# The last 32 keys of four attention units in one batch of scores

## The chip, the cores and the metric

The kernel runs on one core of one Trainium2 chip. What counts is the device time of one execution in microseconds (us), the median of several runs.

## What is computed

Eight images of 256 channels and 32 × 32 positions pass through three layers: an attention over pooled keys and values, a second attention over the tokens, and a gated sum of eight expert networks. Only the first matters here. Each image has 1426 keys at four pooling levels (1024 + 256 + 121 + 25), 8 heads of 32 channels, and 1024 queries:

```python
ks_ = _layernorm(pooled(k_map).transpose(0, 2, 1), norm_w, norm_b)
vs_ = _layernorm(pooled(v_map).transpose(0, 2, 1), norm_w, norm_b)
k = ks_.reshape(B, N, HEADS, DH).transpose(0, 2, 1, 3)
v = vs_.reshape(B, N, HEADS, DH).transpose(0, 2, 1, 3)
attn = jax.nn.softmax(jnp.einsum('bhqd,bhkd->bhqk', q_g, k) * SCALE, axis=-1)
out_att = jnp.einsum('bhqk,bhkd->bhqd', attn, v)
```

All arithmetic is in float32.

## The kernel before

**Units and chunks.** The function `attention` works image by image. An image is four units: two groups `c` of four heads, times two halves of 512 queries. A unit goes through the keys in chunks of `KEY_CHUNKS` (line 44): eleven of 128 keys and one of 18. One chunk is one step, 8 × 4 × 12 = 384 steps in all.

**A step.** `scores` (line 1463) makes four matmuls, one for each head, in four groups of 32 rows of TensorE's array, since a head has 32 channels. They fill the PSUM tile `sc` of four banks, of which there is one. ScalarE writes its exp to a tile `pt` in SBUF, with six buffers. One step later, `values` (line 1473) makes four matmuls in four groups of 32 columns, which add the chunk's part to the PSUM tile `pv`. After every second chunk, `add` (line 1485) lets a DMA on GpSimd's queue add the odd chunk's exp to the even one's in SBUF; VectorE sums these pairs in `sums` (line 1492), and a matmul with ones makes the softmax's denominators of the result.

**What fills TensorE.** While ScalarE does the exp, TensorE works on other things: projections, transposes and the depthwise convolutions' inputs of the next image, and the second attention (`layer1`) of the image before. They are generators, run by a small planner, the class `Flow`. It keeps its own clock for each engine from a table of costs (`cost`), records the instructions in the order in which it runs the generators, and ties them to that order on each engine. After each step it gives out `PACE` us of TensorE time to the first group of generators and `PACE1` to the second (lines 30 and 31, `step` on line 850). `finish` runs whatever is needed until a condition holds, so that a step has its keys, queries and values.

**Keys and values.** `by_tokens` (line 1252) turns four chunks of a map so that tokens lie on partitions, and normalises them; `key_tokens` (line 1427) turns the keys back into `kn`, channels on partitions, three parts for an image. The values remain as `vt`, one tile for every four chunks, so the chunks' borders are those of `KEY_CHUNKS`.

**The main loop** (from line 1812) takes step after step: scores of step `i`, values of step `i - 1`, and filler in between and after. The list it goes through is

```python
steps = [(b, c, half, kc) for b in range(nb) for c in range(2) for half in range(2) for kc in range(NKC)]
```

After the attention, `experts` runs with what is left of `layer1`. Two functions, `layer0_general` and `layer1_general`, stand ready for inputs whose scores are out of bounds; they aren't executed here. Nearly every instruction in the profile has line 669, that of the planner's wrapper, so groups are told apart by tiles: `sc`, `pt`, `pv`, `vt`, `kn`, `q`.

Of the kernel before, what the change touches and what calls it, by code (L numbers as in the profile page):

```python
# [10 lines left out]
AF = mybir.ActivationFunctionType  # L11
# [15 lines left out]
SCALE0 = DH ** -0.5  # L27
SCALE1 = C ** -0.5
FILLER = 5
PACE = 4.0  # L30
PACE1 = 2.0
CAP = (1.5, 1.5)
NEVER = 1e9
MARGIN = 1.5
# [5 lines left out]
NBOUND = 64  # L40
NSTAGED = 64
LIMIT = 1e12
KEY_CHUNKS = [(i * P, min(P, NK - i * P)) for i in range(NKC)]
KEY_SLICES = [(0, 512), (512, 512), (1024, 402)]


# [96 lines left out]
def layer0_general(tc, kit, nb, x, t1, consts, consts8, vecs, q_t, kv_t, proj_t, gqk_t):  # L143
    nc = tc.nc
    T = kit.tile
    with ExitStack() as ctx:
# [189 lines left out]
        def transpose_values(b):  # L336
            acc = vs.pop(b)
            for i in range(0, NKC, 2):
                ps = T(psum, [P, 512], "sm")
                part = KEY_CHUNKS[i : i + 2]  # L340
                for u, (k0, w) in enumerate(part):
                    for c in range(2):
                        o = u * C + c * P
                        nc.tensor.transpose(ps[:w, o : o + P], acc[:, c, k0 : k0 + w], ident)
                whole = [part] if part[-1][1] == P else [part[:1], part[1:]]
                u = 0
                for group in whole:
                    w, g = group[0][1], len(group)
                    src = ps[:w, u * C : (u + g) * C].rearrange("p (a j d) -> p a j d", j=2, d=DH)
                    dst = vext[:w, i + u : i + u + g].rearrange("p u a s d -> p (u a) s d")  # L350
                    nc.vector.tensor_copy(dst[:, :, 0, :], src[:, :, 0, :])
                    nc.scalar.copy(dst[:, :, 2, :], src[:, :, 1, :])
                    u += g

        def global_token(b):
# [19 lines left out]
            yield  # L375
            yield
            ps = T(psum, [P, 512], "sm")
            for kc, (k0, w) in enumerate(KEY_CHUNKS):
                nc.tensor.transpose(ps[:w, kc * 8 : kc * 8 + 8], pg[:, k0 : k0 + w], ident[:HEADS, :HEADS])
            pt = T(work, [P, NKC * 8], "gpt")  # L380
            last, lw = (NKC - 1) * 8, KEY_CHUNKS[-1][1]
            nc.vector.tensor_copy(pt[:, :last], ps[:, :last])
            nc.vector.tensor_copy(pt[:lw, last:], ps[:lw, last : last + 8])
            yield
            yield
            ps = T(psum, [P, 512], "sm")
            for kc, (k0, w) in enumerate(KEY_CHUNKS):
                nc.tensor.matmul(
                    ps[:HEADS, :C],
                    lhsT=pt[:w, kc * 8 : kc * 8 + 8],  # L390
                    rhs=vext[:w, kc, :, 0::2, :],
                    start=kc == 0,
                    stop=kc == NKC - 1,
                )
# [144 lines left out]
        def attend(n, background, steps):  # L539

            pair = n % 4
            qa, ka = qaug.pop(n), kaug[n % 3]
            av = T(work, [P, HW], "av")
            for half in range(2):
                sl = slice(half * 512, half * 512 + 512)
                pv = T(psum, [P, 512], "pv")
                late = None

                def values(kc, w, pt):
                    for j in range(2):  # L550
                        nc.tensor.matmul(
                            pv[64 * j : 64 * j + 64, :],
                            lhsT=vext[:w, kc, pair, j : j + 2, :].rearrange("p s d -> p (s d)"),
                            rhs=pt[:w, j, :],
                            start=kc == 0,
                            stop=kc == NKC - 1,
                        )

                for kc, (k0, w) in enumerate(KEY_CHUNKS):
                    t = T(psum, [P, 2, 512], "sc")  # L560
                    for j in range(2):
                        rows = slice(64 * j, 64 * j + DH + 1)
                        nc.tensor.matmul(
                            t[:w, j, :], lhsT=ka[rows, k0 : k0 + w], rhs=qa[rows, sl], start=True, stop=True
                        )
                    pt = T(work, [P, 2, 512], "pt", bufs=3)
                    nc.scalar.activation(pt[:w], t[:w], AF.Exp, scale=SCALE0)
                    if late is not None:
                        values(*late)
                    late = kc, w, pt  # L570
                    advance(background, steps)
                values(*late)
                nc.vector.tensor_copy(av[:, sl], pv)
            return av
# [81 lines left out]
class Flow:  # L656
# [54 lines left out]
    def cost(self, engine, op, out, ins):  # L711
# [9 lines left out]
        if engine == "PE":  # L721
            if op == "transpose":
                return 0.13
            c = max(0.2, 0.00169 * n)
            return c if self.tiling(ins) is None else c / 4
        psum = any(i.space == PSUM for i in ins)
        if engine == "ACT":
# [150 lines left out]
        return need[0] is not None and (need[2] is None or self.free(need[2]) < NEVER)  # L878


def attention(tc, kit, f, outer, ended, nb, consts, x, t1, t2, hn, bounds, vecs, q_t, kv_t, proj_t, gqk_t, wqk, wqkv, vecs1, w1_d, w1c, gate_d, wrc, vecs2, bnvec):

# [3 lines left out]
    with ExitStack() as ctx:  # L888
# [159 lines left out]
            f.ve.tensor_tensor(bias, ps[:, 0:2], vec[:, V_PB : V_PB + 2], ALU.add)  # L1048

        ks, qs, vts = {}, {}, {}  # L1050
        made = [0]
        turn = [-1]
        todo, done, read, freed, key_parts, normalised = [], [], [4], [0], [0], [0]
# [13 lines left out]
        def until(cond):  # L1067
            return None, cond, None
# [183 lines left out]
        def by_tokens(accs, dst, k0):  # L1252
# [4 lines left out]
            for i in range(0, 4, 2):  # L1257
                span = slice(chunks[i][0], sum(chunks[i + 1]))
                yield pe(*(acc[:, span] for acc in accs), tag="sm")
                ps = small()  # L1260
                for u, (o0, w) in enumerate(chunks[i : i + 2]):
                    for c in range(2):
                        o = u * C + c * P
                        f.pe.transpose(ps[:w, o : o + P], accs[c][:, o0 : o0 + w], ident)
                w = chunks[i + 1][1]
                if w == P:
                    f.act.activation(dst[:, i : i + 2, :], ps.rearrange("p (u c) -> p u c", u=2), AF.Copy)
                else:
                    f.act.activation(dst[:, i, :], ps[:, :C], AF.Copy)
                    f.act.activation(dst[:w, i + 1, :], ps[:w, C:], AF.Copy)  # L1270
            yield ve(dst)
            for u, (_, w) in enumerate(chunks):
                f.ve.bn_stats(st[:w, u, :], dst[:w, u, :])
# [153 lines left out]
        def key_tokens(b, g):  # L1427
# [7 lines left out]
            for c in range(2):  # L1435
                if g == 0:
                    yield until(lambda: turn[0] >= 2 * b - 2 + c)
                    ks[b, c] = T(work, [P, NK], "kn", bufs=3)
                    f.split(ks[b, c], 512, HW)
                yield pe(kt, tag="sm")  # L1440
                ps = small()
                for u, (_, tw) in enumerate(KEY_CHUNKS[4 * g : 4 * g + 4]):
                    f.pe.transpose(ps[:, u * P : u * P + tw], kt[:tw, u, c * P : (c + 1) * P], ident[:tw, :tw])
                f.act.activation(ks[b, c][:, s0 : s0 + w], ps[:, :w], AF.Copy)
            key_parts[0] += 1

# [16 lines left out]
        def scores(b, c, sl, kc):  # L1463
# [6 lines left out]
            f.act.activation(pt[:w], t[:w], AF.Exp, scale=SCALE0)  # L1470
            return pt

        def values(b, c, kc, pt, pv):
            w = KEY_CHUNKS[kc][1]
            for j in range(4):
# [16 lines left out]
        def sums(n, pairs):  # L1492

            for i in range(1, NKC // 2):
                yield until(lambda: len(pairs) > i)
                for j in range(0, 4, 2):
                    s = pairs[0][:, j : j + 2, :]
                    yield ve(s, pairs[i])
                    f.ve.tensor_tensor(s, s, pairs[i][:, j : j + 2, :], ALU.add)
            yield until(lambda: normalised[0] == n)  # L1500
            yield pe(pairs[0], tag="sm")
            total = small()
# [306 lines left out]
        f.finish(lambda: key_parts[0] > 0)  # L1809
        f.spawn(chain(mix(), weights1(), outputs()), 5)  # L1810
        f.spawn(layer1(), 6)
        steps = [(b, c, half, kc) for b in range(nb) for c in range(2) for half in range(2) for kc in range(NKC)]

        pts = {}
        for i in range(len(steps) + 1):
            if i < len(steps):
                b, c, half, kc = steps[i]
                sl = slice(half * 512, half * 512 + 512)
                if kc % 4 == 0:
                    f.finish(lambda: key_parts[0] > 3 * b + kc // 4)  # L1820
# [5 lines left out]
                    f.finish(lambda: {0, 1}.issubset(whole))  # L1826
                if b == 0 and kc == 0:
                    f.finish(lambda: (c, half) in asked)
                pts[i] = scores(b, c, sl, kc)
                f.step()  # L1830
            if i:
                b1, c1, half1, kc1 = steps[i - 1]
                if kc1 == 0:
                    pv = T(psum, [P, 512], "pv")
                    pairs = []
                    sl1 = slice(half1 * 512, half1 * 512 + 512)
                    f.spawn(unit(b1, c1, sl1, i // NKC, pairs), 0)
                f.finish(lambda: kc1 // 4 in vts[b1])
                values(b1, c1, kc1, pts[i - 1], pv)
                if kc1 % 2:  # L1840
                    add(kc1, pts.pop(i - 1), pts[i - 2])
                    pairs.append(pts.pop(i - 2))
                if kc1 == NKC - 1:
                    f.finish(lambda: projected[0] >= b1)
                    f.act.activation(atts[b1, c1][:, sl1], pv, AF.Copy)
# [509 lines left out]
def tile_conv_attn_hybrid(  # L2355
# [45 lines left out]
    with ExitStack() as early:  # L2401
# [3 lines left out]

        ended = [0]
        attention(
            tc, kit, f, (l1, shared), ended, nb,
            consts, x, t1, t2, hn, bounds, vecs0, q_t, kv_t, proj_t, gqk_t, wqk, wqkv, vecs1, w1_d, w1c, gate_d, wrc, vecs2, bnvec,
        )  # L2410
        last(f, (l1, shared), ended, early)
# [122 lines left out]
```

## Time and profile before

The median is 3326.88 us of three runs (3324.67 to 3327.84). The profiled execution spans 3332.1 us.

| engine | busy us | share of the span |
|---|---|---|
| PE (TensorE matmul) | 3137.4 | 94% |
| DVE (VectorE) | 2472.4 | 74% |
| ACT (ScalarE) | 1734.4 | 52% |
| POOL (GpSimd) | 1227.3 | 37% |

The first attention's steps run from 80 to 1970 us, the experts from there to the end. A group line reads: line, engine, operation, output and input tiles, shapes, count, then busy time in us and mean ns of one, then idle time ahead of them and what ended it. `32*128` at a matmul means rows times columns of the array in use. A matmul in float32 is two records. Busy shares are averages over stages with different limits, so they are read by stage.

### The profile page before, as it was taken

Reading aid. Unit: us, or ns where it says so; the run is one execution under the profiler, and the core shown is the slowest. Engines: PE = TensorE matmul, PEld = TensorE weight load, DVE = VectorE, ACT = ScalarE, POOL = GpSimd, SP = SyncE. Lnnn points to the kernel's source line nnn. Section 1 sums busy time; section 2 is a strip of 40 time slices with the busy share of each in tenths; the row PEclk is TensorE's granted clock in tenths of the full one; section 3 lists DMA queues with packets and bytes.
Section 4 is the critical chain, followed back from the end, with each engine's and each line's share of the span. In section 5 each row is a group of like instructions: output and inputs, shape, how many; then the busy total and the mean of one; then the engine's idle time right before and its main releaser. Section 6 shows DMA issues by size and latency. Waiting matters only on the chain.

```text
span 3332.1 us, 42942 instructions
## 1 busy us (share of the span) xinstructions
PE 3137.4 (94%) x15970; PEld 1912.8 (57%) x15970; DVE 2472.4 (74%) x4069; ACT 1734.4 (52%) x2328; POOL 1227.3 (37%) x1300
## 2 busy tenths in 40 slices
PE   8687899999999999899899999999999999999997
PEld 4332244344344344344345346777888888888886
DVE  5687788786887886886884555446998787787776
ACT  4476676666576566576566543333233444444442
POOL 2211413213213214213211112006666776777775
PEclk9798999999999999999999999999999999999999
DMA  2357656656646646656556656124442010000000
GB/s 74 82 121 158 131 106 146 133 101 154 133 100 157 135 104 147 135 120 123 121 125 133 133 119 237 70 88 159 158 146 102 20 45 26 20 20 32 20 13 21
DMA packets 106666, 347.10 MB, mean 104 GB/s; under 512 B 13056, under 2 KB 38408, under 8 KB 83216
## 3 DMA queue, kind: packets, MB, share of 16 engines
q0 software_dynamic: 28608, 179.85, 28.1%
q1 hardware_dynamic: 74480, 162.45, 14.1%
q8 instruction: 128, 2.10, 0.3%
q10 hardware_dynamic: 3360, 1.97, 0.2%
q14 instruction: 90, 0.74, 0.1%
HBM read 105.11 MB, written 73.97 MB: 54 GB/s over the span
## 4 chain that ended last, share of the span: by engine, by line
PE 57%; DVE 5%; issue 3%; ACT 3%; POOL 3%; DMA 2%; SPq 0%; DVEq 0%; POOLq 0%; ACTq 0%
PE bank L669 18%; PE sm L669 13%; PE y L669 8%; PE sc L669 6%; PE sx L669 6%; PE pv L669 5%; DVE h L669 2%; ACT pt L669 2%; POOL tm L669 1%; DVE u L669 1%; DMA pt<-pt 1%; ACT h L669 1%; POOL t L669 1%; DVE t L669 1%; DVE c L669 1%
## 5 line engine op out<-in xcount | busy, mean ns | idle before, releaser
L669 ACT ACTIVATE pt<-sc 128x2048 f32<-128x2048 f32 (+1 forms) x384 | 719.9, 1875 | 326.5 <-PE sc L669 272.7
L669 DVE SCALAR_TENSOR_TENSOR acc<-p,vec,acc 128x225 f32<-128x225 f32 (+7 forms) x928 | 526.6, 574 | 29.3 <-ACT acc L669 4.8
L669 PE MATMUL sc<-q,kn 32*128 32x512 f32 (+1 forms) x3072 | 445.6, 650 | 94.7 <-ACT pt L669 92.9
L669 DVE TENSOR_TENSOR pt<-pt,pt 128x1024 f32<-128x1024 f32 x320 | 387.4, 1254 | 144.3 <-DMA pt<-pt 135.3
L669 POOL DMA_DIRECT2D pt<-pt x192 | 174.0, 907 | 780.1 <-ACT pt L669 615.7
L669 PE MATMUL pv<-pt,vt 128*32 128x512 f32 (+1 forms) x3072 | 420.6, 620 | 0.0
L669 ACT ACTIVATE p1c<-bank 128x256 f32<-128x256 f32 x228 | 87.2, 383 | 576.4 <-PE bank L669 576.1
L669 ACT ACTIVATE h<-h,bnvec 128x512 f32<-128x512 f32 x456 | 345.0, 805 | 50.7 <-DVE h L669 43.7
L669 POOL TENSOR_TENSOR rstd<-rstd,mhalf 128x4 f32<-128x4 f32 (+2 forms) x88 | 107.0, 1216 | 673.8 <-DVE rstd L669 635.0
L669 DVE TENSOR_TENSOR h<-p1c,bank 128x512 f32<-128x512 f32 x228 | 155.2, 681 | 194.7 <-PE bank L669 191.2
L669 PEld LDWEIGHTS sc<-q,kn 32*128 32x128 f32 (+1 forms) x3072 | 116.1, 178 | 285.8 <-ACT pt L669 184.9
L669 POOL TENSOR_TENSOR tm<-h,tm 128x256 f32<-128x256 f32 x206 | 247.6, 1202 | 16.1
L669 DVE TENSOR_TENSOR h<-u,bank 128x256 f32<-128x256 f32 x456 | 232.1, 550 | 7.9
L669 PEld LDWEIGHTS pv<-pt,vt 128*32 128x32 f32 (+1 forms) x3072 | 60.7, 108 | 301.7 <-issue 290.3
L669 POOL TENSOR_TENSOR tm<-h 128x512 f32<-128x512 f32 x103 | 133.9, 1300 | 245.2 <-ACT h L669 241.2
L669 DVE TENSOR_TENSOR h<-h,gate 128x1024 f32<-128x1024 f32 x128 | 209.1, 1642 | 2.5 <-DMA h<-h 2.1
L669 PE MATMUL bank<-h,w2e 128*128 128x256 f32 (+1 forms) x612 | 198.8, 453 | 4.1 <-DVE h L669 4.1
L669 PE MATMUL y<-t,s3e 128*128 128x256 f32 x768 | 188.0, 381 | 10.6 <-POOL t L669 10.3
L669 POOL TENSOR_TENSOR t<-h,t 128x256 f32<-128x256 f32 x210 | 177.4, 845 | 16.5
L669 PE MATMUL bank<-t,s1e 128*128 128x256 f32 x750 | 182.3, 379 | 0.0
L669 PE MATMUL sm<-y,t 128*128 128x256 f32 x752 | 180.6, 385 | 0.0
L669 DVE TENSOR_TENSOR u<-h,bank 128x512 f32<-128x512 f32 x228 | 156.7, 687 | 24.0
(316 smaller groups left out, 5604.3 us busy)
## 6 DMA issues: line engine op xcount, KB each, us to landing
pt<-pt POOLq DMA_DIRECT2D x160, 1024.0 KB, 7.4
h<-h SPq DMA_DIRECT2D x90, 512.0 KB, 3.2
xi<-in_x_dram SPq DMA_DIRECT2D x16, 512.0 KB, 6.7
t<-t SPq DMA_DIRECT2D x8, 1024.0 KB, 9.7
res<-t SPq DMA_DIRECT2D x32, 256.0 KB, 3.9
t<-res SPq DMA_DIRECT2D x32, 256.0 KB, 5.4
hn<-res SPq DMA_DIRECT2D x32, 256.0 KB, 3.0
hn<-hn SPq DMA_DIRECT2D x16, 512.0 KB, 4.2
```

The source lines that it names most:

```text
L669: ins = fn(*args, **kwargs)
```

## The change

The last chunk has only 18 keys and costs a whole step. The change makes the last chunk 32 keys and the one ahead of it 114, and computes the last chunk's scores for all four units of an image at once, in unit 0's last step. There 16 matmuls of 32 rows and 32 columns use every combination of row group (head) and column group (unit), so that the four units' scores lie on four groups of 32 partitions of one `sc` tile. One exp serves them all. Unit 0 uses its part from SBUF. The parts of units 1 to 3 are stored to DRAM tiles `last0` to `last2`, and each is fetched to partitions 0 to 31 of a `pt` buffer when its unit is at its third last chunk. Units 1 to 3 then have 11 steps instead of 12, and the last one makes the values of both its chunks. The rest follows from that: the planner's paces rise to 4.3 and 2.15, its cost of the 16 matmuls is a sixteenth each, the functions that never run keep the old chunks as `WHOLE_CHUNKS`, and sums take only the rows of a pair.

```diff
-PACE = 4.0
-PACE1 = 2.0
+PACE = 4.3
+PACE1 = 2.15
...
-KEY_CHUNKS = [(i * P, min(P, NK - i * P)) for i in range(NKC)]
+WHOLE_CHUNKS = [(i * P, min(P, NK - i * P)) for i in range(NKC)]
+LAST = 32
+KEY_CHUNKS = [(i * P, P) for i in range(NKC - 2)]
+KEY_CHUNKS += [((NKC - 2) * P, NK - LAST - (NKC - 2) * P), (NK - LAST, LAST)]
...
+            if self.key(out).startswith("sc") and ins[0].shape[-1] == LAST:
+                return c / 16
...
+        lasts = [kit.tile(dram, [LAST, 4, 512], f"last{n}") for n in range(3)]
...
+        def last_scores(b):
+            k0 = KEY_CHUNKS[-1][0]
+            t = T(psum, [P, 4, 512], "sc")
+            for n in range(4):
+                c, half = divmod(n, 2)
+                for j in range(4):
+                    r = slice(DH * j, DH * j + DH)
+                    f.pe.matmul(
+                        t[LAST * n : LAST * n + LAST, j, :],
+                        lhsT=ks[b, c][r, k0:],
+                        rhs=qs[b, c][r, half * 512 : half * 512 + 512],
+                        start=True,
+                        stop=True,
+                    )
+            pt = T(work, [P, 4, 512], "pt", bufs=6)
+            f.act.activation(pt, t, AF.Exp, scale=SCALE0)
+            for n in range(1, 4):
+                f.sp.dma_start(lasts[n - 1], pt[LAST * n : LAST * n + LAST])
+            return pt
+
+        def fetch_last(n):
+            pt = T(work, [P, 4, 512], "pt", bufs=6)
+            f.sp.dma_start(pt[:LAST], lasts[n - 1])
+            return pt
...
-                    s = pairs[0][:, j : j + 2, :]
+                    s = pairs[0][:w, j : j + 2, :]
...
-        steps = [(b, c, half, kc) for b in range(nb) for c in range(2) for half in range(2) for kc in range(NKC)]
+        steps = [
+            (b, n, kc) for b in range(nb) for n in range(4) for kc in range(NKC if n == 0 else NKC - 1)
+        ]
...
-                pts[i] = scores(b, c, sl, kc)
+                if kc == NKC - 1:
+                    f.finish(lambda: (b, 1) in qs and (b or len(asked) == 4))
+                    pts[n, kc] = last_scores(b)
+                else:
+                    pts[n, kc] = scores(b, c, sl, kc)
+                if n and kc == NKC - 3:
+                    pts[n, NKC - 1] = fetch_last(n)
                 f.step()
...
-                values(b1, c1, kc1, pts[i - 1], pv)
-                if kc1 % 2:
-                    add(kc1, pts.pop(i - 1), pts[i - 2])
-                    pairs.append(pts.pop(i - 2))
+                for kc1 in (kc1, NKC - 1) if n1 and kc1 == NKC - 2 else (kc1,):
+                    f.finish(lambda: kc1 // 4 in vts[b1])
+                    values(b1, c1, kc1, pts[n1, kc1], pv)
+                    if kc1 % 2:
+                        add(kc1, pts.pop((n1, kc1)), pts[n1, kc1 - 1])
+                        pairs.append(pts.pop((n1, kc1 - 1)))
```

## What the prediction was

> **What bounds the kernel now.** I read the time line of the span in 40 slices first, then busy time by stage, then the groups of instructions with their shapes kept apart, the views of the tiles `sc` and `pt`, TensorE's order of work in one stretch, and the DMA issues.
>
> ```profile
> PE   8687899999999999899899999999999999999997
> DVE  5687788786887886886884555446998787787776
> ACT  4476676666576566576566543333233444444442
> ```
>
> ```profile
> 1043.00:1283.00 240.00, 231.94 (x1321) 109.44 (x1320) 195.21 (x348) 156.82 (x193) 59.91 (x72) 1.00 0.60 130
> 1283.00:1526.00 243.00, 232.66 (x1318) 108.92 (x1320) 194.47 (x349) 156.06 (x193) 61.92 (x72) 0.99 0.58 124
> 1976.00:3332.00 1356.00, 1309.47 (x5782) 1088.48 (x5781) 987.22 (x1409) 496.25 (x821) 760.32 (x737) 0.99 0.21 74
> ```
>
> The columns are span, then busy time of PE, weight load, DVE, ACT and POOL, then clock, DMA share and GB/s. An image of the first attention takes about 240 us, of which PE works 232 (97%), DVE 195 (81%), ACT 157 (65%). ACT, which loses most of the work below, is not the limit; PE is, and DVE is next. The experts after 1976 us are PE-bound as well, and the change doesn't touch their formulas.
>
> ```profile
> 508.27 1.14 PE L669 MATMUL sc<-q,kn 32*128 32x512 f32 x8
> 509.34 1.06 PE L669 MATMUL pv<-pt,vt 128*32 128x512 f32 x8
> 510.33 1.99 PE L669 MATMUL sx<-y,t 128*128 128x256 f32 x8
> 512.26 1.07 PE L669 MATMUL sm<-pt,con 128*32 128x512 f32 x8
> ```
>
> This is one step of `attention`: scores from 508.27 to 509.34 (1.07 us), values to 510.33 (0.99), filler (here layer 1's) after that. Eight records are four matmuls, two passes each. Filler of this shape takes 1.73 us when more of its kind follows (the chain of waits has such pieces), 1.93 here, so a change into full-array work and out of it costs 0.20.
>
> ```profile
> L669 PE MATMUL sc<-q,kn x3072: 587/599/1218, 79.9 to 1968.6; 32*128 32x512 f32 x192
> ...
>   DMA pt<-pt: 17.5, 9
> ...
>   PE sc L669: 92.9, 92
> ```
>
> 3072 records are 384 steps in 1889 us, 4.92 us each. In the list of what ended idle time before work on `sc`, a DMA on a `pt` buffer accounts for 17.5 us, 9 times (exps that had no buffer); in the list of who waited, PE's scores stood 92.9 us for `sc` to be read, less than 5% of the stage.
>
> ```profile
> L669 ACT ACTIVATE pt<-sc 18x2048 f32<-18x2048 f32 x32 | 59.7, 1864 | 27.6 <-PE sc L669 24.3 <-issue 2.9 <-DVE acc L669 0.4
> L669 PE MATMUL sc<-q,kn 32*18 32x512 f32 x256 | 34.0, 600 | 12.6 <-ACT pt L669 12.6
> ```
>
> The last 18 keys cost what 128 cost: exp 1864 ns against 1876, matmul 600 ns against 655. That is the waste the change goes for.
>
> ```profile
> pt<-pt POOLq DMA_DIRECT2D x160, 1024.0 KB, 7.4
> ...
> res<-t SPq DMA_DIRECT2D x32, 256.0 KB, 3.9
> ...
> hn<-pool SPq DMA_DIRECT2D x28, 256.0 KB, 2.8
> ```
>
> An addition of one chunk's exp into its neighbour takes 7.4 us to land, a 256 KB load 3.9, a 256 KB store 2.8.
>
> [...] The trace shows four concurrent, in rows and in columns (1.07 and 0.99 us for four); no run here shows sixteen. [...]
>
> **The change part by part.**
>
> *Removed steps.* Units 1 to 3 of each image lose their last step: 8 × 3 = 24 score batches and 24 exps. PE saves 24 × 1.07 = 25.7 us. The values of those keys remain, but now directly behind those of chunk 10, in the same tiling, and the removed step's filler joins filler elsewhere. I take 0.3 us per step for that: 0.20 for the change into filler and out[...]. 24 × 0.3 = 7.2, so PE loses 32.9 us. ACT loses 24 × 1.876 = 45 us, which lies beside PE and counts for nothing by itself.
>
> *The common batch.* Unit 0's last step becomes 16 matmuls of 32 × 32 with 512 columns. If all run together, 1.07 us plus small start offsets, the cost of the batch it replaces. If the four groups of units run one after the other, 4 × 1.07 = 4.28. [...] I take 1.3, since four distinct operands are already streamed at once today, by the values: 8 × 0.23 = 1.8 us lost. The ends are 0 and 8 × 3.21 = 25.7.
>
> *DRAM round trip.* 48 transfers of 256 KB, 12.6 MB, beside some 236 MB that 125 GB/s make over 1889 us: DMA engines are about 60% busy, so there is room. A store lands in 2.8 us, and its first reader comes nine or ten steps later, over 40 us. A fetch is issued at chunk 9's step and needed two steps later, behind two score batches and two value batches: about 2 × 4.92 + 2 = 11.8 us against 3.9. Hidden, unless its issue waits. [...]
>
> *Buffers.* `pt` has six. The fetch takes one at chunk 9, where the last exp took one two steps later, so chunk 10's exp gets the buffer of chunk 7, which is free once the addition of 6 and 7 has landed. That is issued behind step 8's values: start of step 8 + 2.1 + 0.9 (issue) + 7.1 (the tile's median) = 10.1 us. The exp wants it two steps + 1.1 later: 10.9 us at 4.92 per step, no wait; but 7.5 us in steps of 3.2, the shortest that scores and exp allow: a wait of 2.6. The built order shows that units 1 and 2 of images 2 to 7 now get little filler (by the durations above about 19 and 15 us of it in 11 steps). I take 0.5 us on 12 such units, 6 us; the ends are 0 and 2.6 on each of 24 units, 62.
>
> *Order of filler.* The pace per step rises by 7.5% for 6% fewer steps. In the built order TensorE reaches the first expert matmul at the same place, with the same layer-1 work ahead of it but for four matmuls of 256 columns, and one plain expert product becomes a seven-product one: under 2 us, counted as nothing. Chunk widths of 114 and 32 in place of 128 and 18 change no duration[...] (18 rows against 128 above).
>
> *First image.* Its steps wait for the maps, not for PE (between 80 and 330 us PE works 191 of 250): half of its 3 × 1.37 is lost, 2 us.
>
> Sum: 32.9 − 1.8 − 6 − 2 = 23.1. 3326.9 − 23.1 = 3303.8, forecast 3304.
>
> **The rivals.**
> - *More than that, 3291.* In 9 of 32 units the last step ended with scores waiting at once for its exp, a step of 3.2 us where PE had 2.1 of work. Removing such a step saves 1.1 more: 24 × 9/32 × 1.1 = 7, and if the buffers cost nothing, 13 in all. For it: ACT is relieved. Against: the values that remain, and buffers.
> - *The 16 matmuls don't overlap, 3328.* 4.28 each instead of 1.3: 24 us back, almost the whole gain. [...] For it: no row of this trace has both groups in use. [...]
> - *Buffers or fetches become the wait, 3336.* Units 1 and 2 of every image lose 2.4 at chunk 10: 16 × 2.4 = 38 in place of 6. For it: exps already wait for additions 9 times. Against: the schedule knows the buffers and can put filler there. This one is slower than before.
>
> **How the numbers follow.** Forecast 0.58, the larger gain 0.16, no overlap 0.10[...], buffers or fetches 0.16. The range takes in the larger gain with 7 us to spare and stops short of the two bad cases: 3284 to 3324. It leaves out most of 0.05 + 0.13, and a little below. Faster by over 0.2% (under 3320): 0.58 + 0.16 + 0.05 and a small part of the rest, 0.80. Within: 0.07. Slower (over 3333): 0.13.
>
> **What would show it.** Steps: 360 exps, the last common one as long as the others (1.88); 16-matmul batches about 1.1 to 1.3 us from their start to the values; PE's busy time down by about 30 us and the images of the steady state at some 237 us; the experts' stage still 1356. Against it: batches over 2 us; exps waiting for DMA on `pt` much more than 17.5 us; value matmuls that wait for `pt<-last`; PE idle of an image well over 8 to 10 us.

## The result, and the profile after

The changed kernel takes 3371.07 us (median of four runs, 3363.09 to 3379.95) against 3325.78 for the kernel before in the same session: a ratio of 1.0137, 95% interval 1.0105 to 1.0169. It is 45 us slower; the forecast was 23 us faster, and the range, 3284 to 3324, missed it.

The page of the changed kernel, engines and slices (its lines are numbered three higher, L672 for L669):

```profile
PE 3134.3 (93%) x15976; PEld 1919.5 (57%) x15976; DVE 2479.1 (73%) x4070; ACT 1696.6 (50%) x2305; POOL 1214.0 (36%) x1306
...
PE   8687898889989989999989898999999999999997
DVE  5687777697877877886975453445998778777776
ACT  4476663666566566566565552333223444444432
```

TensorE was to lose about 30 us of busy time and lost 3.1 (3137.4 to 3134.3), and the digits of its row drop to 8 more often up to slice 24. Two things hide in that. Busy time counts a matmul at half clock about double (16 value records take 3.80 us at half clock and 2.06 elsewhere, below), so I split the span into three parts: idle (span less PE busy), the time lost to half clock (half of the busy time of PE in which the record of the granted clock shows 0.5), and what remains, the net work. Half clock in which PE is idle anyway adds nothing to its busy time and isn't counted: of 178.8 us at half clock after the change, PE was busy in 132.4; before, in 92.6 of 128.6.

| us | before | after | difference |
|---|---|---|---|
| net work (busy less lost) | 3091.0 | 3068.1 | −22.9 |
| lost to half clock | 46.3 | 66.2 | +19.9 |
| idle of TensorE | 194.7 | 243.8 | +49.1 |
| span of the profiled run | 3332.1 | 3378.1 | +46.0 |

Both profiled runs are about 9 us longer than the medians, so their difference can stand for that of the medians. Work went, as forecast, if less of it. It came back as idle time and as time at half clock, three times over. By stage, the changed kernel (images 1, 2, 4 and 5 of the first attention, then the experts; columns as in the prediction: span, then busy PE, weight load, DVE, ACT, POOL, clock, DMA share, GB/s):

```profile
322.00:593.00 271.00, 239.54 (x1317) 112.62 (x1320) 202.29 (x358) 152.24 (x190) 74.16 (x92) 0.95 0.58 127
593.00:820.00 227.00, 202.40 (x1164) 81.46 (x1164) 176.14 (x312) 148.32 (x181) 45.85 (x55) 0.95 0.63 135
1057.00:1302.00 245.00, 231.96 (x1317) 108.84 (x1318) 198.52 (x343) 151.57 (x190) 60.73 (x73) 0.99 0.65 140
1302.00:1546.00 244.00, 229.81 (x1310) 108.02 (x1314) 192.47 (x337) 149.78 (x189) 55.61 (x72) 0.98 0.62 132
2002.00:3378.00 1376.00, 1329.02 (x5871) 1101.10 (x5869) 996.07 (x1419) 503.87 (x831) 763.60 (x745) 0.99 0.22 73
```

The same view of the kernel before, images 1 and 2:

```profile
330.00:558.00 228.00, 211.32 (x1194) 87.66 (x1198) 182.12 (x323) 151.47 (x179) 60.51 (x72) 0.96 0.62 136
558.00:798.00 240.00, 228.26 (x1298) 105.29 (x1291) 191.23 (x337) 155.57 (x192) 58.03 (x66) 0.99 0.60 129
```

Images 1 and 2 took 468 us and take 498. Image 1 holds 123 matmul records more than before (1317 against 1194, the counts in brackets), image 2 has 134 fewer: filler has moved between images. Idle in the two rose from 28.4 to 56.1 us (span less PE busy of each image, from its first score to the next image's), and their clock fell (0.96 and 0.99 before, 0.95 and 0.95 after). The experts' row can't be held against the 1356 us of the prediction, because the two stretches begin at different places. Counted from the end of the last scores, this stage rose from 1363 to 1375 us: TensorE has 44 matmul records more there, nearly all of them moved from the attention, at the same idle time (46.6 and 47.0). In image 1 the fourth unit alone lasts 109.8 us, 55.6 before. TensorE's time line at its end in the changed kernel (start, duration, what; in brackets the idle time ahead and what ended it):

```profile
568.25 0.28 PE L672 MATMUL sm<-dev,con 128*128 128x2 f32 x2
573.87 1.22 PE L672 MATMUL sm<-s,con 128*128 128x256 f32 x2 [5.33 <-DVE s L672]
574.88 8.52 PE L672 MATMUL sm<-p,v 128*128 128x256 f32 x32
583.24 0.60 PE L672 MATMUL sx<-con,acc 128*128 128x128 f32 x4
583.68 0.60 PE L672 MATMUL sm<-con,acc 128*128 128x128 f32 x4
584.76 0.89 PE L672 MATMUL sx<-con,res 128*128 128x128 f32 x4 [0.48 <-ACT kt L672]
590.03 2.81 PE L672 MATMUL sm<-con,kt 128*128 128x128 f32 x8 [4.37 <-ACT kt L672]
592.76 2.09 PE L672 MATMUL sc<-q,kn 32*128 32x512 f32 x8
```

The last scores ahead of these started at 539.00 us, so none runs for over 53 us: `finish` runs whatever leads to image 2's keys, because the next step needs them. The chain through VectorE and ScalarE leaves TensorE idle for 5.33 and 4.37 us, and the next scores run at half clock (2.09 us from start to end against 1.14). In the built order image 2's maps begin 12 steps into image 1 here and 9 steps in before, and the last of them stands 5 steps ahead of image 2 (before: 14). Such a lead of the maps over their image can be read from an order before it runs, and it went with the long unit in all 20 traces of this document: from image 2 on, the unit ahead of an image lasted 104 to 131 us in the 12 cases in which the last map stood 6 steps ahead or fewer, and at most 82 us in all others. In four orders of 384 steps the lead was never under 11. The other images lost less each, 23 us of idle in images 3 to 7 together (46.1 to 69.4).

The view of the tile `sc` after the change:

```profile
L672 PE MATMUL sc<-q,kn x3072: 587/612/1218, 79.2 to 2003.0; 32*128 32x512 f32 x160, 32*114 32x512 f32 x16, 32*32 32x512 f32 x16
L672 ACT ACTIVATE pt<-sc x360: 1850/1878/1936, 82.4 to 2003.7; 128x2048 f32<-128x2048 f32 x164, 114x2048 f32<-114x2048 f32 x16
...
  DMA pt<-pt: 51.2, 17
  DVE pt L672: 23.1, 10
...
  PE sc L672: 111.4, 99
```

There are 360 exps, each as long as before (1878 ns in the middle, 1877 before). Exps that had to wait for a DMA on a buffer rose from 17.5 us to 51.2, and PE's scores stood 111.4 us for `sc` instead of 92.9. How such a wait reaches TensorE shows in ScalarE's and TensorE's time lines of one stretch:

```profile
1424.94 1.88 ACT L672 ACTIVATE pt<-sc 114x2048 f32<-114x2048 f32 x1 [3.20 <-DMA pt<-pt]
1428.21 1.88 ACT L672 ACTIVATE pt<-sc 128x2048 f32<-128x2048 f32 x1 [1.39 <-PE sc L672]
```

```profile
1421.80 1.13 PE L672 MATMUL sc<-q,kn 32*114 32x512 f32 x8 [0.41 <-ACT pt L672]
1422.86 1.06 PE L672 MATMUL pv<-pt,vt 128*32 128x512 f32 x8
1426.87 1.29 PE L672 MATMUL sc<-q,kn 32*128 32x512 f32 x8 [2.95 <-ACT pt L672]
1428.10 3.80 PE L672 MATMUL pv<-pt,vt 114*32 114x512 f32 x16
```

The exp of the 114 keys waits for a buffer until an addition has landed, the scores wait 2.95 us for that exp, and the next 16 value records take 3.80 us where they take 2.06 elsewhere: they run at half clock, in a piece of 6.83 us that begins at 1427.7. In the record of the changed kernel's granted clock, half clock comes in 31 pieces: 19 of 3.41 us, nine of 6.83, and one each of 10.24, 17.09 and 27.31. Five idle stretches of 2.9 to 3.3 us in this trace, the one shown among them, came with half clock that began between 1.1 us before their end and 1.5 us after it.

### The profile page after: what moved, and what is told of

It reads as the page before. It is cut to its first block, busy times and chain, and to the rows that moved or that the text cites. A ratio compares the mean times of both kernels' runs of the same rounds, so it can differ in the third digit from the quotient of the medians.

```text
span 3378.1 us, 43085 instructions
## 1 busy us (share of the span) xinstructions
PE 3134.3 (93%) x15976; PEld 1919.5 (57%) x15976; DVE 2479.1 (73%) x4070; ACT 1696.6 (50%) x2305; POOL 1214.0 (36%) x1306
## 5 line engine op out<-in xcount | busy, mean ns | idle before, releaser
L672 ACT ACTIVATE pt<-sc 128x2048 f32<-128x2048 f32 (+1 forms) x360 | 676.0, 1878 | 310.6 <-PE sc L672 215.7
L672 DVE SCALAR_TENSOR_TENSOR acc<-p,vec,acc 128x225 f32<-128x225 f32 (+7 forms) x928 | 528.4, 577 | 31.3 <-ACT acc L672 6.3
L672 PE MATMUL sc<-q,kn 32*128 32x512 f32 (+2 forms) x3072 | 425.2, 656 | 115.6 <-ACT pt L672 111.4
L672 DVE TENSOR_TENSOR pt<-pt,pt 128x1024 f32<-128x1024 f32 (+1 forms) x320 | 386.3, 1253 | 155.3 <-DMA pt<-pt 140.8
L672 POOL DMA_DIRECT2D pt<-pt x192 | 170.6, 890 | 852.2 <-ACT pt L672 652.7
L672 PE MATMUL pv<-pt,vt 128*32 128x512 f32 (+2 forms) x3072 | 423.3, 626 | 9.0 <-DMA pt<-last 9.0
L672 ACT ACTIVATE p1c<-bank 128x256 f32<-128x256 f32 x229 | 88.0, 384 | 579.1 <-PE bank L672 578.7
L672 ACT ACTIVATE h<-h,bnvec 128x512 f32<-128x512 f32 x458 | 347.5, 807 | 56.4 <-DVE h L672 48.7
L672 POOL TENSOR_TENSOR rstd<-rstd,mhalf 128x4 f32<-128x4 f32 (+2 forms) x88 | 99.5, 1131 | 661.0 <-DVE rstd L672 575.7
L672 DVE TENSOR_TENSOR h<-p1c,bank 128x512 f32<-128x512 f32 x229 | 156.1, 682 | 187.4 <-PE bank L672 186.9
L672 PEld LDWEIGHTS sc<-q,kn 32*128 32x128 f32 (+2 forms) x3072 | 114.0, 179 | 311.5 <-ACT pt L672 208.3
L672 POOL TENSOR_TENSOR tm<-h,tm 128x256 f32<-128x256 f32 x208 | 247.4, 1189 | 16.3
L672 PEld LDWEIGHTS pv<-pt,vt 128*32 128x32 f32 (+2 forms) x3072 | 61.2, 109 | 316.6 <-issue 289.9
L672 DVE TENSOR_TENSOR h<-u,bank 128x256 f32<-128x256 f32 x458 | 233.3, 550 | 7.9
L672 POOL TENSOR_TENSOR tm<-h 128x512 f32<-128x512 f32 x104 | 134.7, 1295 | 248.1 <-ACT h L672 248.0
L672 DVE TENSOR_TENSOR h<-h,gate 128x1024 f32<-128x1024 f32 x128 | 209.7, 1647 | 1.1 <-DMA h<-h 0.6
L672 PE MATMUL bank<-h,w2e 128*128 128x256 f32 (+1 forms) x608 | 197.6, 453 | 5.5 <-DVE h L672 4.2
L672 PE MATMUL y<-t,s3e 128*128 128x256 f32 x768 | 187.9, 381 | 9.9 <-POOL t L672 9.8
L672 PE MATMUL sm<-p,v 128*128 128x256 f32 x832 | 194.4, 385 | 0.0
L672 PE MATMUL sm<-y,t 128*128 128x256 f32 x760 | 181.5, 386 | 4.2 <-ACT sm L672 4.0
L672 PEld LDWEIGHTS sm<-p,v 128*128 128x128 f32 x832 | 156.1, 191 | 49.9 <-issue 30.1
L672 POOL TENSOR_TENSOR t<-h,t 128x256 f32<-128x256 f32 x212 | 178.2, 841 | 16.6
```

The lines of the kernel that those rows point to most:

```text
L672: ins = fn(*args, **kwargs)
```

## The experiments

The first theory was that the loss comes from what surrounds the last 32 keys of units 1 to 3: transfers, a sixth of the buffers, or their 256 KB addition behind that of chunk 9. (The kernel before makes the addition of the last chunk too, 32 times with 144 KB, but each in a step of its own.) The rival was that the new order of filler costs. Eighteen kernels tell them apart; all medians are in the table at the end of this part.

**1. Transfers, order and paces.** `e1_no_fetch` drops stores, fetches and the addition that uses them; the values of these keys run on other data of the same shape:

```diff
-            for n in range(1, 4):
-                f.sp.dma_start(lasts[n - 1], pt[LAST * n : LAST * n + LAST])
...
-                if n and kc == NKC - 3:
-                    pts[n, NKC - 1] = fetch_last(n)
...
+                    if n1 and kc1 == NKC - 1:
+                        other = vts[b1][2].rearrange("p (j u) c -> p j (u c)", u=2)
+                        values(b1, c1, kc1, other, pv)
+                        pairs.append(pts.pop((n1, kc1 - 1)))
+                        continue
```

> Leaves out the stores to and fetches from DRAM of units 1 to 3, and the addition of their last 32 keys into the neighbouring pair; the value matmuls of these keys still run, with other data of the right shape. TensorE's work is that of the changed kernel. Theory 'buffers' (a fetched tile takes a pt buffer early, so exps wait for additions and sums, TensorE idles and its clock drops): 3300 to 3315, exps waiting for DMA or DVE under 25 us. Theory 'schedule' (fewer steps and the new pace make the next image's keys late, whatever the buffers): over 3340, image 1 again some 270 us.

3322.96 us, ratio 0.9984 (0.9977 to 0.9991). So 48 us hang on what was left out, or on the order that goes with it; and even without all of it the change brings 5 us and not the forecast's 23.

`e2_after_pace4` has the changed kernel at the old paces, `e3_before_pace43` the kernel before at the new ones:

```diff
-PACE = 4.3
-PACE1 = 2.15
+PACE = 4.0
+PACE1 = 2.0
```

> The changed kernel with the old paces, 4.0 and 2.0. Theory 'schedule': the pace is the cause, 3300 to 3325, image 1 back to some 230 us. Theory 'buffers': 3355 to 3380, the exps still waiting some 50 us or more for buffers.

> The kernel before with the new paces, 4.3 and 2.15. Theory 'schedule' in its form that the pace is the cause: 3345 or more. Theory 'buffers': 3315 to 3335, no difference.

3357.77 and 3329.77: the pace alone moves the changed kernel by 13 us and the one before by nothing that these runs can tell. `e4_fetch_late` fetches one step later, and holds the buffer for one step less:

```diff
-                if n and kc == NKC - 3:
+                if n and kc == NKC - 2:
```

> The fetch is issued one step later, with chunk 10's scores instead of chunk 9's, so its buffer is held about 4.5 us less, and it has some 7 us instead of 11 to land. Theory 'buffers': 3335 to 3355. Theory 'schedule': no difference, 3360 to 3380. If fetches get late: values wait for pt<-last over 30 us in sum, and it is slower than 3380.

3379.03: no gain from the shorter hold. TensorE, VectorE and ScalarE run the same order as in the changed kernel, and exps wait less for a DMA on a buffer (39.9 us against 51.2), yet it is no faster.

**2. One part at a time.** `e5_transfers_only` keeps the stores and puts a copy from DRAM to DRAM in each fetch's place, with no buffer and no addition. `e6_buffer_only` has no transfers, but takes the buffer, fills it and adds it. `e7_no_last_add` has everything but the addition. `e8_fetch_pool` moves the fetch to GpSimd's queue.

```diff
 e5
-            f.sp.dma_start(pt[:LAST], lasts[n - 1])
+            f.sp.dma_start(spare[n - 1], lasts[n - 1])
 e6
-            f.sp.dma_start(pt[:LAST], lasts[n - 1])
+            f.pool.memset(pt[:LAST], 1.0)
 e7
-                        add(kc1, pts.pop((n1, kc1)), pts[n1, kc1 - 1])
+                        odd = pts.pop((n1, kc1))
+                        if n1 == 0 or kc1 < NKC - 1:
+                            add(kc1, odd, pts[n1, kc1 - 1])
 e8
-            f.sp.dma_start(pt[:LAST], lasts[n - 1])
+            f.pool.dma_start(pt[:LAST], lasts[n - 1])
```

> As the run without fetches, but the 24 stores are made, and 24 copies of the same size on the same queue at the same places go from DRAM to DRAM instead of into a pt buffer; the values of the last 32 keys of units 1 to 3 read other data and their addition is left out. Theory 'buffers': the transfers are harmless, 3318 to 3330 like the run without fetches. Theory 'transfers' (their traffic or SP's blocked queue): 3350 or more.

> The changed kernel without stores and fetches: the pt buffer is taken at the same place and filled with ones by GpSimd, so the data of units 1 to 3 is other data; the addition of these keys is made. Theory 'buffers' (or the addition that comes with them): 3350 to 3380. Theory 'transfers': 3318 to 3335.

> The changed kernel with stores and fetches, but the addition of the last 32 keys into their pair is left out in units 1 to 3, so sums miss these keys. The fetched buffer is then free as soon as the values have read it, some 8 us earlier, and the last pair needs no transfer. If what is costly is the time that the fetched buffer is held, addition included: 3320 to 3340, and image 2's keys are made in time as in the run without fetches. If it is the buffer at chunk 10's exp alone: 3350 or more.

> The changed kernel with the fetch on GpSimd's queue instead of SP's. Theory 'SP's blocked queue': 3330 or less. Theory 'buffers': no gain, 3360 to 3385.

3322.95, 3360.08, 3327.10 and 3373.91. The transfers cost nothing (e5 against e1's 3322.96), buffer and fetch some 4 us (e7 against e5, whose intervals overlap). Everything with the addition was slow and everything without it was not, so it seemed to be the cause.

**3. Made, or only told.** The addition acts in two ways: the chip makes it, and the planner sets its clocks by it. `e9_add_untold` makes it but doesn't tell the planner; `e10_add_told_only` sets the clocks as if it were made (a pair ready 1.0 + 1.5 + 0.0078 × 256 us later) and leaves it out; `e11_untold_pace4` is e9 at the old paces.

```diff
 e9
-            f.pool.dma_start(
+            (nc.gpsimd if untold else f.pool).dma_start(
 e10
+                        else:
+                            f.pretend(odd[:LAST], pts[n1, kc1 - 1][:LAST])
```

> The changed kernel in full, additions included, but the addition of the last 32 keys of units 1 to 3 isn't recorded with the planner, so the order of all other instructions is that of the run without it (image 2's maps start 36 steps ahead of it, not 33). Theory 'order' (what the planner makes of the later pair is what costs): 3320 to 3335. Theory 'held buffer' (the addition on the chip holds the buffer and the pair): 3355 or more.

> The reverse: the addition of the last 32 keys in units 1 to 3 is left out, but the planner's clocks are set as if it were made, so that the order is that of the changed kernel (image 2's maps 33 steps ahead). Theory 'order': 3350 to 3380, with a unit of some 109 us ahead of image 2. Theory 'held buffer': 3320 to 3335.

> As the changed kernel with the untold addition, with the old paces 4.0 and 2.0. In this order image 3's maps are made late (the last 5 steps ahead of it). Theory 'order': a long unit of over 95 us ahead of image 3, none ahead of image 2, and 3335 to 3365. If late maps aren't what costs: as with the new paces, 3320 to 3335.

3362.34, 3361.20 and 3399.73. TensorE's, VectorE's and ScalarE's built orders are the same in e1, e5, e7 and e9, so e9 against e7 is the addition alone, in an order that doesn't expect it: +35 us. And e10, which does nothing on the chip that e7 doesn't do, is 34 us slower: that is order alone. The two don't add up in the changed kernel (+44).

The traces allow a closer comparison. Into image 5, e10 has the very order of the changed kernel on TensorE, VectorE and ScalarE, and lacks only the addition. Idle and lost time up to the first scores of image 5 are 149.7 us in e7, 188.4 in e10 and 200.1 in the changed kernel; e4 and e8, which have its order and its addition, stand at 205.1 and 191.8. So in this stretch the changed kernel's order costs 39 us against e7's, and the addition 3 to 17 more (each from one profiled run).

**4. Earlier, or on VectorE.** If lateness was the point, the same addition made earlier should be cheap. `e12_add_early` fetches at chunk 6, makes the last keys' values with chunk 8 and adds them there, so that chunk 10 has no addition behind it; `e13_add_early_pace415` is that at paces of 4.15 and 2.1. `e14_add_dve` has no addition by DMA there: VectorE takes the last keys as a seventh pair.

```diff
 e12
-                if n and kc == NKC - 3:
+                if n and kc == NKC - 6:
...
+                if n1 and kc1 == NKC - 4:
+                    values(b1, c1, NKC - 1, pts[n1, NKC - 1], pv, False)
+                    add(NKC - 1, pts.pop((n1, NKC - 1)), pts[n1, kc1])
 e14
-            for i in range(1, NKC // 2):
+            for i in range(1, NKC // 2 + (n % 4 > 0)):
...
+                    if n1 and kc1 >= NKC - 2:
+                        pairs.append(pts.pop((n1, kc1)))
```

> Whole computation. Units 1 to 3 fetch their last 32 keys three steps earlier, make their values with chunk 8 and add them to chunk 8 there, so that chunk 10 forms the last pair alone, with no addition behind it. If the late addition into the last pair is what costs: near the kernel without it, 3322 to 3335. If the held buffer and its fetch cost whatever their place: the buffer is held for three steps more, exps wait for DMA more than in the changed kernel, 3360 to 3385. If any addition of these keys costs the same: about 3360.

> The kernel before this in the list, with paces of 4.15 and 2.1. If the place of the addition decides: within 10 us of it, and both under 3340. If the order that the planner happens to find decides: the two differ by 15 us or more, in either direction.

> Whole computation. Units 1 to 3 leave out the addition by DMA of the last 32 keys; VectorE adds them as a pair of their own, 24 x 2 adds of 1.15 us more, 55 us in 8 images or 7 us an image where VectorE has 45 us to spare. If the landing of a late DMA addition costs: 3325 to 3340, with no wait of VectorE for a DMA on the last pair. If a late last pair costs whatever its means, or VectorE's added work does: 3350 or more.

3358.34, 3355.94 and 3366.22. My theory of the late addition falls. After its first image e12 has no unit of over 71 us, so the long unit isn't needed for the loss either; its idle time is spread over all images. e13, another order, lies within 3 us of e12, where 15 or more was expected if the order decides: between these two it didn't.

**5. The same work in other orders.** That left a suspicion: e1, e5 and e7 are one and the same order, so three good results were one. `e15_no_add_pace40` and `e16_no_add_pace415` are e7, without the addition, in two other orders; `e17_before_pace415` and `e18_before_pace385` are the kernel before in two other orders.

```diff
 e15
-PACE = 4.3
-PACE1 = 2.15
+PACE = 4.0
+PACE1 = 2.0
 e16, e17
+PACE = 4.15
+PACE1 = 2.1
 e18
+PACE = 3.85
+PACE1 = 1.9
```

> The kernel without the addition of the last 32 keys in units 1 to 3 (its denominators lack them), with paces of 4.0 and 2.0. If the addition is what costs: within 10 us of 3327. If the three fast kernels share a fortunate order: 3345 to 3370, as the kernels with the addition.

> As the kernel ahead of it, without the addition of the last 32 keys in units 1 to 3, with paces of 4.15 and 2.1. If the addition costs: within 10 us of 3327. If it is the order: 3345 to 3370, and it needn't agree with the kernel at 4.0.

> The kernel before with paces of 4.15 and 2.1. If the 384-step form is robust: 3322 to 3335, as with 4.0 and 4.3. If orders scatter in this form as well, and its paces were tuned to a fortunate one: 3340 or more.

> The kernel before with paces of 3.85 and 1.9. If the 384-step form is robust: 3322 to 3340. If orders scatter in this form as well: 3340 or more.

e15 settles one thing: without the addition, and with nothing changed against e7 but two numbers of the planner, the time is 3377.45, 50 us more and as long as the changed kernel's. The addition isn't needed for the loss. e16 alone would have spoken for the addition, since it stayed within 10 us of e7, and of the two orders of the kernel before one scattered (3347.70) and one didn't (3332.28). TensorE's time line of e15 at the end of image 2, whose fourth unit lasts 130.8 us, shows what the changed kernel shows in image 1:

```profile
814.26 1.22 PE L672 MATMUL sm<-s,con 128*128 128x256 f32 x2 [4.61 <-DVE s L672]
815.28 7.98 PE L672 MATMUL sx<-p,v 128*128 128x256 f32 x32
826.37 0.90 PE L672 MATMUL sm<-con,res 128*128 128x128 f32 x4 [3.11 <-issue]
832.12 1.22 PE L672 MATMUL sm<-diag,con 128*128 128x256 f32 x2 [4.85 <-POOL diag L672]
...
847.78 1.95 PE L672 MATMUL sm<-con,kt 128*128 128x128 f32 x4 [3.24 <-ACT kt L672]
...
850.52 2.09 PE L672 MATMUL sc<-q,kn 32*128 32x512 f32 x8
```

The maps of the image to come are 5 steps ahead of it in the built order, as in the changed kernel, `finish` makes the rest in one piece, and the scores after it run at half clock (2.09 us from start to end).

All runs, with the split of the profiled one:

| kernel | steps | median us | ratio (95% interval) | net work | idle | lost to half clock |
|---|---|---|---|---|---|---|
| before | 384 | 3325.78 | | 3091.0 | 194.7 | 46.3 |
| e3 | 384 | 3329.77 | 1.0003 (0.9993 to 1.0012) | 3091.8 | 195.8 | 41.7 |
| e18 | 384 | 3332.28 | 1.0015 (1.0006 to 1.0023) | 3095.2 | 191.7 | 36.4 |
| e17 | 384 | 3347.70 | 1.0058 (1.0037 to 1.0078) | 3091.7 | 203.0 | 49.3 |
| e5, no addition | 360 | 3322.95 | 0.9985 (0.9972 to 0.9999) | 3068.3 | 209.0 | 42.8 |
| e1, no addition | 360 | 3322.96 | 0.9984 (0.9977 to 0.9991) | 3068.7 | 208.2 | 40.8 |
| e7, no addition | 360 | 3327.10 | 0.9993 (0.9983 to 1.0002) | 3069.3 | 210.7 | 42.7 |
| e16, no addition | 360 | 3334.82 | 1.0016 (1.0006 to 1.0026) | 3066.2 | 217.3 | 54.9 |
| e10, no addition | 360 | 3361.20 | 1.0098 (1.0081 to 1.0115) | 3068.4 | 232.8 | 56.5 |
| e15, no addition | 360 | 3377.45 | 1.0150 (1.0128 to 1.0172) | 3070.9 | 245.7 | 58.1 |
| e13 | 360 | 3355.94 | 1.0079 (1.0062 to 1.0096) | 3065.8 | 228.2 | 62.9 |
| e2 | 360 | 3357.77 | 1.0087 (1.0060 to 1.0113) | 3068.6 | 232.9 | 54.4 |
| e12 | 360 | 3358.34 | 1.0098 (1.0081 to 1.0115) | 3067.5 | 233.3 | 53.2 |
| e6 | 360 | 3360.08 | 1.0084 (1.0060 to 1.0108) | 3068.9 | 231.3 | 56.2 |
| e9 | 360 | 3362.34 | 1.0107 (1.0090 to 1.0124) | 3071.3 | 234.8 | 51.2 |
| e14 | 360 | 3366.22 | 1.0113 (1.0096 to 1.0129) | 3071.3 | 247.5 | 45.1 |
| after | 360 | 3371.07 | 1.0137 (1.0105 to 1.0169) | 3068.1 | 243.8 | 66.2 |
| e8 | 360 | 3373.91 | 1.0140 (1.0122 to 1.0157) | 3068.3 | 244.3 | 54.7 |
| e4 | 360 | 3379.03 | 1.0151 (1.0130 to 1.0172) | 3067.9 | 244.5 | 62.7 |
| e11 | 360 | 3399.73 | 1.0211 (1.0194 to 1.0229) | 3073.4 | 253.4 | 73.7 |

Net work has two values: 3091 to 3095 with 384 steps, 3066 to 3073 with 360. Everything else is idle time and half clock: 228 to 252 us in four orders of the 384-step form, 249 to 327 in those of the 360-step form. The order that e1, e5 and e7 share gives back 8 to 12 us of the saving against the kernel before (idle and lost time of 249.0 to 253.4 against 241.0), e16 31, and the others 45 or more. The split is that of one run, which for e18 is 7 us shorter than the median.

## Why the prediction was wrong

*Removed steps: right in kind, too large.* 32.9 less 1.8 for the common batch makes 31.1 us of TensorE's work; the net work fell by 22.9, and by 23.5 between the means of the two forms. The scores alone are 25.7 of the forecast, so nothing of the other 7.2 is seen: 0.20 us a step of it was read from one stretch of the trace, and the rest was my estimate.

*Common batch: right, and cheaper than the 1.3 taken.* The changed kernel's TensorE time line:

```profile
1370.74 1.14 PE L672 MATMUL sc<-q,kn 32*32 32x512 f32 x32
1371.81 1.08 PE L672 MATMUL pv<-pt,vt 114*32 114x512 f32 x8
```

Sixteen matmuls take 1.07 us to the next work (1.07 to 1.08 in all eight batches), as four do (1.07). The rival without overlap is out.

*DRAM round trip: nearly right.* The list of DMA issues, with the median us from issue to landing, and the tile view of `last`:

```profile
pt<-pt POOLq DMA_DIRECT2D x32, 256.0 KB, 4.5
...
last<-pt SPq DMA_DIRECT2D x24, 256.0 KB, 4.6
pt<-last SPq DMA_DIRECT2D x24, 256.0 KB, 4.8
```

```profile
  PE pv L672: 9.0, 3
```

A store took 4.6 us and not 2.8, a fetch 4.8 and not 3.9, and the values waited for one three times, 9.0 us in all, which the forecast put at nothing. e5 makes 48 transfers in these places at no cost (3322.95 against e1's 3322.96).

*Buffers and addition: the mechanism is there, the addition's size was wrong.* I took 6 us. Exps' waits for additions rose by 33.7, near the 38 of the rival that ended at 3336. But e16 shows what such a row is worth:

```profile
  DMA pt<-pt: 51.7, 21
```

It has as much of it as the changed kernel and ends at 3334.82; e6 has 25.4 and ends at 3360.08. So this row doesn't rank the kernels. The addition itself costs more than the 6 in two orders, held fixed on TensorE, VectorE and ScalarE, that don't expect it: 35 us in e9 against e7, 22 in e11 against e15. In e9 that isn't by exps waiting longer for a DMA (37.0 us, 38.6 in e7); which wait it is isn't shown.

*Order of filler: the step that failed.* I compared where attention ends and what stands ahead of it, found a difference of under 2 us there and counted it as nothing; how filler lies within the stage got no term at all. Against 22.9 us of work saved there are 69 us more of idle (49.1) and half clock (19.9). What the order has in it shows up to image 5: the changed kernel's order costs 39 us there against e7's, and the addition 3 to 17. With it fell the silent assumption that in a stage in which TensorE is 97% busy a us of its work is a us of time. It holds only while filler is spread as well as before. e7, e15 and e16 do the same work (net work of 3066.2 to 3070.9) with three spreads, and lie up to 50 us apart; e7 and e10 differ in nothing but the spread either, and lie 34 apart. How the loss against the kernel before divides between order and addition over the whole span isn't shown, since no run has that order without the addition to the end. The built order, which I had, showed image 2's maps 5 steps ahead of it where they had been 14.

*What stays open.* Why the orders of the 360-step form are worse on the whole isn't shown. They have less room in a unit (11 steps for the same filler), their maps stand closer to their image, and the exps mostly wait more for buffers (25 to 84 us, against 14 to 30 in four orders of the 384-step form), but no run varies any of these alone. e12 and e13, where every map stands 7 steps ahead or more, are nearly as slow as the others with the addition, so late maps are one way to lose and not the only one. No version with the whole computation was found that beats the kernel before; other orders of the changed kernel weren't searched on the chip.

## What to carry to other kernels

Where a planner or scheduler lays out the work, a change of the work is also a change of the order, and the second can be worth more than the first: measure the scatter over a few harmless settings, of both forms, before one result is taken for the worth of the change. Split a span into net work, idle time and time lost to half clock (only where the engine is busy); a busy row mixes the first and the last. Look in the built order for work that a coming stage needs and that stands just ahead of it. And when several experiments agree, see whether they share an order: they may be one sample.

## What the runs showed of the hardware

Sixteen matmuls on all 32 × 32 parts of the array took 1.07 us to the next work, as four did in four groups of 32 rows (1.07). From 130 us on, TensorE was idle for 2.9 us or more 14 times in the changed kernel's trace, and half clock began within 2 us of the end of each stretch, or inside it; three of these are shown above (2.95, 4.37 and 5.33 us, then 6.83 us of half clock each, from 1427.7, 588.1 and 571.0). In the kernel before one such stretch of six, of 3.23 us, had no half clock after it. How much half clock goes with idle time isn't fixed: 49 us more of idle went with 20 us more lost in the changed kernel, and 53 us more with none in e14 (45.1 us lost against 46.3). In one pair of the same TensorE order (e7 and e9), 24 additions of 256 KB by DMA, which took 4.6 us in the middle, cost 35 us (3362.34 against 3327.10) where the order doesn't expect them.
